# First attention layer of an eight-layer hybrid network: two-part normalization, loads in another order and in slices, and TensorE's transposes and products in groups of one or two steps

## The chip, the cores and the metric

The kernel runs on one core of one Trainium2 chip. The metric is the device time of one execution in microseconds (us): the median of several runs. A separate execution is recorded by the hardware profiler, and every duration below comes from that one execution unless it is called a median. A core has five engines that run side by side, each taking its own queue of instructions in order: TensorE (PE, matrix products and transposes, with PEld for its weight loads), VectorE (DVE), ScalarE (ACT), GpSimd (POOL) and SyncE (SP, which only issues transfers here). Transfers (DMA) run on 16 DMA engines, which all issuing queues share. TensorE writes only to PSUM; VectorE and ScalarE copy its results out to SBUF.

## The reference, cut to what matters

The network is eight layers with residuals on an input x of 4 sequences x 1024 positions x 128 features, all in float32. The change concerns the first layer, a causal attention with 16 heads of 64 features:

```python
x = x + _L0_attn_a_ref(_layernorm(x, axis=-1), Wq, Wk, Wv, Wo, bo)
...
def _L0_attn_a_ref(x, Wq, Wk, Wv, Wo, bo):
    q = split_heads(x @ Wq)
    k = split_heads(x @ Wk)
    v = split_heads(x @ Wv)
    scores = jnp.einsum('bhid,bhjd->bhij', q * beta, k)
    ...
    scores = jnp.where(causal, mask_value, scores)
    attn = jax.nn.softmax(scores, axis=-1)
    out = jnp.einsum('bhij,bhjd->bhid', attn, v)
    out = out.transpose(0, 2, 1, 3).reshape(b, n, INNER)
    return out @ Wo + bo
```

After it come a mixture of experts, a gated attention, the mixture again, a state-space layer, a gated feed-forward layer, a second attention and the feed-forward layer again. Their arithmetic does not change.

## The kernel before, in words

**The constructors load the weights.** `LOADS` (L1706) lists the layers in the order in which their constructors run. Nearly all loads go to SP's queue. `GatedAttention.relative_bias` (L802) builds a table through a round trip to DRAM: POOL fills `rel_row`, SP writes it out (L823) and reads it back shifted (L825). `GatedFFN.scaled` loads three integer weights, each into a short-lived buffer, and POOL converts them (L1286). The short-lived buffers reuse each other's memory, and the attention's working tiles come to lie on it too. `load_late` (L91) puts the mixture's two large weights W1 and W2 (2 MB each) in a list `k.late`, after one exponential of the state-space layer; the attention issues the whole list on ACT's queue (L371 to L375) when it has reached query group 2 of the first pair of heads.

**Units.** The attention works on 32 pairs of heads: 4 sequences x 8 pairs. The 1024 queries of a pair are cut into four groups `gq` = 0 to 3 of two blocks of 128 (`Q` = 2, `NQ` = 4). Being causal, group `gq` needs the first 2(gq+1) key blocks, so its second stage has gq+1 *steps* of two key blocks. That makes 10 steps a pair, and 36 pairs of (key block, query block) on or under the diagonal, of which a step holds 4, or 3 on the diagonal.

**First stage**, `probabilities` (L336), a generator: for each query block, matrix products give the scores `s` of both heads (L352, each head on its 64 rows of the array); DVE adds the mask, writes `p` and finds the maximum (L358, and L365 if there were two tiles); ACT takes the exponential and its sum (L367). After the second block of a unit DVE takes the reciprocal `r` of the sums (L380). The factors are then needed along another axis: SP writes `r` to DRAM (L383) and reads it back, broadcast, with two transfers (L386) into `share`.

**Second stage**, `outputs` (L414): in each step, TensorE transposes the two key blocks of `p` (L426, into tiles `t`), DVE and ACT copy one each to `pt` (L433, L431), and `product` (L447) multiplies by the values (L451, each head into its 64 columns of the array) and sums in `o`; after the last step DVE multiplies `o` by `share` (L458). The products of a step are kept in `waiting` and issued one step later.

**Small work**, `pieces`: projections of a later pair (`projected`, L265: two features each of q and k, evacuated by ACT at L282 and by DVE at L284, and four pieces of values for every second pair, L291, evacuated by L107 and L109 in turn), the output projection of the pair before (`joined`, L306), and the turning of the normalized input (L260). All of them use one PSUM tile, `m` of pool `ps_m`. `outputs` issues one piece in each step. `ahead` (L402) then runs the first stage until it is `LEAD` = 20 blocks ahead.

So TensorE's order, which is written out by hand (`pe` pins it), is in each step: transposes, one piece, scores, products of the step before. `ve` pins the order of DVE's score reductions; other instructions are placed in their engine's queue by a scheduler, which can deviate from the order of the source. [...]in tiles of 128 x 512 float32, `ps_s` has 2 x 2, `ps_t` 2 x 1, `ps_o` and `ps_m` one each, eight in all.

**Between sequences**, `normalized(b)` (L248) is called two pairs before the next sequence begins: `normalize` (L111) does the statistics (L117, L119) on DVE, a square root on ACT (L121), then reciprocal and scaling on DVE (L122, L124), and appends the two pieces that turn the result.

Of the kernel before, what the change touches and what calls it, by code (L numbers as in the profile page):

```python
# [11 lines left out]
F32 = mybir.dt.float32  # L12
# [8 lines left out]
P = 128  # L21
B = 4
# [39 lines left out]
class Kernel:  # L62


    def __init__(self, ctx: ExitStack, tc: tile.TileContext, ins: dict, out):
# [5 lines left out]
        self.got = ctx.enter_context(tc.tile_pool(name="got", bufs=GOT))  # L71
# [19 lines left out]
    def load_late(self, pool, name, shape, src):  # L91

        t = pool.tile(shape, F32, name="w_" + name)
        self.late.append(lambda: self.nc.scalar.dma_start(t, src))
        return t
# [15 lines left out]
    def normalize(self, out, in_, n=NC, pin=lambda ins: ins):  # L111
# [9 lines left out]
        nc.scalar.activation(rstd, mv[:, :, 1], AF.Sqrt, bias=self.eps)  # L121
        pin(nc.vector.reciprocal(rstd, rstd))  # L122
# [72 lines left out]
class AttentionA:  # L195
# [10 lines left out]

    Q = 2
    NQ = NC // 2
    LEAD = 20
# [11 lines left out]
    def __call__(self, start=None):  # L221
# [4 lines left out]
        with self.stack as ctx:  # L226
# [4 lines left out]
            ps_s = ctx.enter_context(tc.tile_pool(name="a_ps", bufs=2, space=PSUM))  # L231
            ps_t = ctx.enter_context(tc.tile_pool(name="a_pt", bufs=2, space=PSUM))
# [12 lines left out]
            xts, pairs, units = {}, {}, {}  # L245
            pieces = []

            def normalized(b):  # L248
                xl = one.tile([P, NC, C], F32, tag="xl", name="xl")
                k.normalize(xl, k.xb(b), pin=ve)  # L250
                nc.gpsimd.tensor_tensor(
                    k.xb(b), k.xb(b), bo.unsqueeze(1).to_broadcast([P, NC, C]), ALU.add
                )

# [81 lines left out]
            def probabilities(n, gq):  # L336
# [7 lines left out]
                for i in range(Q):  # L344
# [67 lines left out]
            waiting = []  # L412

            def outputs(n, gq):  # L414


                p, share = units.pop((n, gq))
                last = (gq + 1) * Q - 1
                for step in range(gq + 1):
                    products = []  # L420
                    for jb in (2 * step, 2 * step + 1):
                        lo = max(0, jb * P - gq * Q * P)
                        t = ps_t.tile([P, 2, Q * P], F32, tag="t", name="t")
                        for h in range(2):
                            for i in range(lo // P, Q):
                                pe(nc.tensor.transpose(  # L426
                                    t[:, h, i * P : (i + 1) * P], p[:, h, i, jb * P : (jb + 1) * P], k.ident
                                ))
                        pt = sb.tile([P, 2, Q * P], F32, tag=f"pt{jb % 2}", name="pt")
                        if jb % 2:  # L430
                            nc.scalar.copy(pt[:, :, lo:], t[:, :, lo:])  # L431
                        else:
                            nc.vector.tensor_copy(pt[:, :, lo:], t[:, :, lo:])  # L433
                        products.append((jb, lo, pt))
                    done[1] += 4 if step < gq else 3
                    if pieces:
                        pieces.pop(0)[1]()
                    ahead()
                    while waiting:
                        waiting.pop(0)()  # L440
                    if step == 0:
                        o = ps_o.tile([P, Q * P], F32, tag="o", name="o")
                    waiting.append(
                        lambda products=products, step=step: product(n, gq, o, share, products, last, step == gq)
                    )

            def product(n, gq, o, share, products, last, at_end):  # L447
                for jb, lo, pt in products:
                    for h in range(2):
                        feats = slice(h * DH_A, (h + 1) * DH_A)  # L450
                        pe(nc.tensor.matmul(  # L451
                            o[feats, lo:], pairs[n]["v"][:, jb, feats], pt[:, h, lo:],
                            start=jb == 0, stop=jb == last,
                        ))
                if at_end:
                    if gq == 0:
                        pairs[n]["o"] = sb.tile([P, T], F32, tag="ot", name="ot")
                    nc.vector.tensor_tensor(  # L458
                        pairs[n]["o"][:, gq * Q * P : (gq + 1) * Q * P], o, share, ALU.mult
                    )  # L460

            normalized(0)
# [12 lines left out]
            while waiting:  # L475
                waiting.pop(0)()
# [8 lines left out]
class Mixture:  # L485
# [7 lines left out]
    def __init__(self, k: Kernel):  # L493
# [15 lines left out]
        self.place = w.tile([P, CAP], F32, name="place")  # L509
        nc.gpsimd.iota(  # L510
            self.place, [[1, CAP]], base=0, channel_multiplier=0, allow_small_or_imprecise_dtypes=True
        )
# [10 lines left out]
    def __call__(self, start=None):  # L523
# [1310 lines left out]
```

## Time and profile before

| | us |
|---|---|
| median of 3 runs (3391.43 to 3402.13) | 3398.55 |
| the profiled execution, total | 3378.53 |
| its span, from the first to the last instruction | 3376.7 |
| last product of the first attention (L451) starts | 1214.03 |

The profiled execution is 20.0 us, or 0.6%, quicker than the median of the runs.

| stretch of the span | length | PE busy | DVE busy | ACT busy | granted TensorE clock |
|---|---|---|---|---|---|
| 0 to 30 us | 30 | 15.77 | 11.03 | 9.17 | 1.00 |
| 100 to 200 us | 100 | 100.00 | 68.47 | 53.73 | 1.00 |
| 500 to 600 us | 100 | 96.21 | 69.23 | 53.51 | 0.97 |
| 800 to 900 us | 100 | 95.03 | 70.86 | 54.40 | 0.98 |

The busy times are sums over the instructions of an engine in the stretch. TensorE's ends are modelled, so that instructions of a run overlap in the record and "100.00" says that there is always some instruction, not that the array computes all the time; the distance from one start to the next is what is measured. The clock is the mean share of full speed that the throttle granted. A line of an engine's timeline gives start, length, engine, line, operation, output<-input, count, and in brackets the idle time before it with what ended it.

### The profile page before, as it was taken

To read this page: it belongs to the slowest core of one execution; us is meant where nothing else is said; L and a number is where in the kernel's file an instruction comes from. 1 tells how busy PE (TensorE), PEld (TensorE's weight loads), DVE (VectorE), ACT (ScalarE), POOL (GpSimd) and SP (SyncE) were. 2 spreads that over 40 slices of the span, in tenths; PEclk is the share of its full clock that TensorE was granted. 3 is DMA by queue.
4 is the path that set the end of the run, shared out by engine and by line. 5 is a ranking of instruction groups with operands and counts; after the bars stand their busy time and mean duration, and the time that the engine had idled before them with its cause. 6 is when DMAs were issued, how large, how long until landed. Compare 5 with 4: busy or idle time off the path is not lost.

```text
span 3376.7 us, 45533 instructions
## 1 busy us (share of the span) xinstructions
PE 3015.2 (89%) x16624; PEld 1655.0 (49%) x16624; DVE 2306.0 (68%) x5281; ACT 1812.9 (54%) x3819; POOL 273.0 (8%) x269
## 2 busy tenths in 40 slices
PE   5999999999999979869988597978778799999988
PEld 2555555555455547635566344444445344444435
DVE  3666666666776656666566589897977677677634
ACT  2555555555555523445423597979654265556662
POOL 1000000000000002530013200000001101010000
PEclk8999999999999989989999798989999699899999
DMA  5110111111110101100001111111111112121100
GB/s 156 16 16 14 15 18 16 14 17 17 14 17 15 15 8 32 53 10 1 0 16 40 53 64 50 57 57 51 63 38 42 34 44 53 31 51 31 30 2 25
DMA packets 149537, 109.35 MB, mean 32 GB/s; under 512 B 91760, under 2 KB 130432, under 8 KB 146880
## 3 DMA queue, kind: packets, MB, share of 16 engines
q1 hardware_dynamic: 128352, 72.84, 9.4%
q0 software_dynamic: 17408, 27.32, 3.3%
q10 hardware_dynamic: 3552, 6.29, 0.6%
q8 instruction: 130, 2.13, 0.4%
q14 instruction: 95, 0.78, 0.1%
HBM read 90.76 MB, written 15.60 MB: 31 GB/s over the span
## 4 chain that ended last, share of the span: by engine, by line
PE 68%; DVE 11%; ACT 8%; DMA 6%; issue 6%; POOL 1%; SPq 0%; DVEq 0%; ACTq 0%; POOLq 0%
PE s L352 8%; PE t L426 8%; PE o L451 8%; PE acc L649 4%; PE o L1613 4%; PE acc L1227 4%; PE x L1579 3%; PE ps L280 3%; PE acc L948 3%; PE s L1515 3%; ACT p L1585 3%; DMA shares<-r 2%; ACT hc L1226 2%; DVE st L1214 2%; DVE tops L1524 2%
## 5 line engine op out<-in xcount | busy, mean ns | idle before, releaser
L358 DVE CUSTOM_DVE_ANT_0 p<-s,mask 128x512 f32<-128x512 f32 (+3 forms) x768 | 394.6, 553 | 170.5 <-PE s L352 168.3
L367 ACT ACTIVATE p<-p,tops 128x640 f32<-128x640 f32 (+7 forms) x512 | 391.7, 767 | 146.1 <-DVE tops L365 85.4
L1585 ACT ACTIVATE p<-x 128x512 f32<-128x512 f32 (+3 forms) x768 | 337.6, 490 | 246.4 <-PE x L1584 176.6
L1524 DVE TENSOR_REDUCE tops<-s 128x2 f32<-128x1024 f32 (+3 forms) x384 | 361.3, 956 | 133.8 <-PE s L1520 94.2
L431 ACT COPY pt<-t 128x512 f32<-128x512 f32 (+1 forms) x320 | 157.7, 493 | 380.0 <-PE t L426 379.5
L1227 PE MATMUL acc<-hc,ident 128*128 128x512 f32 x512 | 270.1, 652 | 93.2 <-ACT hc L1226 92.3
L352 PE MATMUL s<-kt,qt 64*128 64x512 f32 (+3 forms) x1536 | 339.4, 533 | 2.7 <-DVE tops L358 2.6
L451 PE MATMUL o<-pt,vv 128*64 128x256 f32 (+1 forms) x2560 | 323.3, 374 | 14.7 <-ACT pt L431 9.4
L426 PE MATMUL t<-ident,p 128*128 128x128 f32 x2304 | 326.2, 282 | 3.7 <-DVE pt L433 3.0
L426 PEld LDWEIGHTS t<-ident,p 128*128 128x128 f32 x2304 | 248.1, 142 | 103.3 <-issue 70.0
L1214 DVE TENSOR_TENSOR_SCAN st<-decay,st 128x1024 f32<-128x1024 f32 x128 | 288.8, 2279 | 10.9 <-ACT decay L1211 10.4
L451 PEld LDWEIGHTS o<-pt,vv 128*64 128x64 f32 x2560 | 156.6, 137 | 263.9 <-issue 157.3
L433 DVE COPY pt<-t 128x512 f32<-128x512 f32 x320 | 220.0, 687 | 66.0 <-PE t L426 66.0
L1579 PE MATMUL x<-q,k 75*128 75x512 bf16 (+3 forms) x768 | 223.1, 338 | 27.7 <-ACT p L1585 15.0
L1515 PE MATMUL s<-k,q 72*128 72x512 bf16 (+3 forms) x768 | 216.3, 348 | 31.9 <-DVE tops L1524 17.6
L1226 ACT ACTIVATE hc<-ps,by_time 128x256 f32<-128x256 f32 x512 | 200.7, 478 | 50.6 <-PE ps L1220 50.5
L352 PEld LDWEIGHTS s<-kt,qt 64*128 64x128 f32 x1536 | 112.5, 188 | 180.7 <-issue 139.7
L1227 PEld LDWEIGHTS acc<-hc,ident 128*128 128x128 f32 x512 | 91.7, 198 | 209.6 <-ACT hc L1226 191.0
L738 POOL DMA_INDIRECT got<-y_rows,rows x128 | 136.7, 1068 | 645.1 <-DMA y_rows<-y 543.5
L1213 DVE TENSOR_TENSOR st<-du,bs 128x1024 f32<-128x1024 f32 x128 | 151.8, 1217 | 49.4 <-PE ps L1220 49.2
L649 PE MATMUL acc<-d,xl 128*128 128x480 f32 (+1 forms) x384 | 152.8, 559 | 26.2 <-DVE d L644 26.2
L1220 PEld LDWEIGHTS ps<-ident,st 128*128 128x128 f32 x1024 | 126.0, 146 | 96.5 <-issue 60.7
(272 smaller groups left out, 4740.7 us busy)
## 6 DMA issues: line engine op xcount, KB each, us to landing
bs<-b_rows SPq DMA_DIRECT2D x64, 512.0 KB
share<-shares SPq DMA_DIRECT2D x256, 64.0 KB
k<-b_parts POOLq DMA_DIRECT2D x16, 576.0 KB, 13.2
q<-b_parts POOLq DMA_DIRECT2D x48, 192.0 KB, 12.1
b_parts<-part SPq DMA_DIRECT2D x24, 256.0 KB
y_rows<-y SPq DMA_DIRECT2D x16, 192.0 KB
x<-in_x_dram SPq DMA_DIRECT2D x4, 512.0 KB
w_W<-in_W_dram ACTq DMA_DIRECT2D x1, 2048.0 KB
```

The lines of the kernel that those rows point to most:

```text
L352: pe(nc.tensor.matmul(s[:, h, : hi - lo], q[feats, ib * P : (ib + 1) * P], kk[feats, lo:hi], start=True, stop=True,))
L358: ve(nc.vector.tensor_tensor_reduce(p[:, h, i, lo:hi], s[:, h, : hi - lo], m, -1.0, 3.4e38, ALU.add, ALU.min, tops[:, h, i, at : at + 1],))
L367: exp = nc.scalar.activation(p[:, h, i, :width], p[:, h, i, :width], AF.Exp, bias=tops[:, h, i, 0:1], scale=-1.0, accum_out=sums[:, h, i : ...
L426: pe(nc.tensor.transpose(t[:, h, i * P : (i + 1) * P], p[:, h, i, jb * P : (jb + 1) * P], k.ident))
L451: pe(nc.tensor.matmul(o[feats, lo:], pairs[n]["v"][:, jb, feats], pt[:, h, lo:], start=jb == 0, stop=jb == last,))
L649: pe(nc.tensor.matmul(acc[n][:, :m, :].rearrange("p e s -> p (e s)"), xl[:, c, :], d[:, e : e + m, :].rearrange("p e s -> p (e s)"), start ...
L1214: nc.vector.tensor_tensor_scan(st, decay, st, 0.0, ALU.mult, ALU.add)
L1227: nc.tensor.matmul(acc[:, c : c + 2, :].rearrange("p c d -> p (c d)"), k.ident, hc.rearrange("p c d -> p (c d)"), start=n == 0, stop=n == ...
L1515: start.pin(nc.tensor.matmul(s[:, a, : hi - lo], qq[:ROWS, two + a, ib * P : (ib + 1) * P], kk[:ROWS, two + a, lo:hi], start=True, stop=ha ...
L1524: nc.vector.tensor_reduce(tops[:, half, two : two + 2, n], s[:, :, : hi - lo], AX.X, ALU.max)
L1579: start.pin(nc.tensor.matmul(x[:, lo:], kk[:FULL, a, jb * P : (jb + 1) * P], qq[:FULL, a, hq * 512 + lo : (hq + 1) * 512], start=True, sto ...
L1585: nc.scalar.activation(p[:, a, lo:], x[:, lo:], AF.Exp)
```

## The change

The diff has these parts. `normalize` becomes a generator `normal` with a break after the square root; in the attention, statistics and root run three pairs ahead at `gq` 1, the scaling at `gq` 2, and the two turning pieces (`across`) are appended where the whole was before. `GatedFFN` moves ahead of `GatedAttention` in `LOADS`. `load_late` makes one transfer for each of the 8 experts instead of one for all, and one entry of the list is issued at the end of each unit from unit 2 on. In the second stage, transposes and products come in groups, `GROUPS`: six a pair instead of ten steps. A group issues a piece, all its transposes, another piece, the products of the group before, and then calls `ahead`. The transposed tiles, now of two key blocks, share a ring of three buffers with the scores (`ps_s` with 3 x 2 tiles, `ps_t` gone), and the copies `pt` have 4 buffers for each of their two tags instead of 2. The mixture's gather buffers and its table `place` move from the constant pool into the mixture's own pools.

```diff
@@ Kernel
-        self.got = ctx.enter_context(tc.tile_pool(name="got", bufs=GOT))
...
-        self.late.append(lambda: self.nc.scalar.dma_start(t, src))
+        self.late.extend(
+            lambda at=at: self.nc.scalar.dma_start(t[:, at], src[:, at]) for at in range(shape[1])
+        )
...
-    def normalize(self, out, in_, n=NC, pin=lambda ins: ins):
+    def normalize(self, out, in_, n=NC):
+        for _ in self.normal(out, in_, lambda ins: ins, n):
+            pass
+    def normal(self, out, in_, pin, n=NC):
...
         nc.scalar.activation(rstd, mv[:, :, 1], AF.Sqrt, bias=self.eps)
+        yield
         pin(nc.vector.reciprocal(rstd, rstd))
@@ AttentionA
+    GROUPS = [[(0,)], [(0, 1)], [(0,), (1, 2)], [(0, 1), (2, 3)]]
...
-            ps_s = ctx.enter_context(tc.tile_pool(name="a_ps", bufs=2, space=PSUM))
-            ps_t = ctx.enter_context(tc.tile_pool(name="a_pt", bufs=2, space=PSUM))
+            ps_s = ctx.enter_context(tc.tile_pool(name="a_ps", bufs=3, space=PSUM))
...
-                k.normalize(xl, k.xb(b), pin=ve)
+                parts = k.normal(xl, k.xb(b), ve)
+                next(parts)
+                yield
+                for _ in parts:
+                    pass
...
-                    if k.late and gq == 2:
+                    if k.late and i == Q - 1 and n * NQ + gq > 1:
                         pin = k.order()
                         pin(exp)
-                        while k.late:
-                            pin(k.late.pop(0)())
+                        pin(k.late.pop(0)())
...
             def outputs(n, gq):
                 p, share = units.pop((n, gq))
+                for steps in self.GROUPS[gq]:
+                    piece()
+                    blocks = [block for step in steps for block in turned(p, gq, step)]
+                    piece()
+                    while behind:
+                        behind.pop(0)()
+                    if steps[0] == 0:
+                        o = ps_o.tile([P, Q * P], F32, tag="o", name="o")
                     ahead()
+                    behind.append(lambda blocks=blocks: products(n, gq, o, share, blocks))
...
+            def turned(p, gq, step):
+                t = ps_s.tile([P, 2, 2, Q * P], F32, tag="s", name="t")
...
+                    blocks.append((jb, lo, sb.tile([P, 2, Q * P], F32, tag=f"pt{m}", name="pt", bufs=4)))
+                for m, (jb, lo, pt) in enumerate(blocks):
+                    if m:
+                        nc.scalar.copy(pt[:, :, lo:], t[:, m, :, lo:])
+                    else:
+                        nc.vector.tensor_copy(pt[:, :, lo:], t[:, m, :, lo:])
+                done[1] += 4 if step < gq else 3
...
                 for gq in range(NQ):
+                    if gq == 1 and n + 3 < B * NP and (n + 3) % NP == 0:
+                        normal = normalized((n + 3) // NP)
+                    if 0 < gq < 3:
+                        next(normal, None)
                     if gq == 0 and n + 2 < B * NP and (n + 2) % NP == 0:
-                        normalized((n + 2) // NP)
+                        across((n + 2) // NP)
@@ Mixture
-        self.place = w.tile([P, CAP], F32, name="place")
...
+            many = ctx.enter_context(tc.tile_pool(name="m_got", bufs=GOT))
...
+            place = one.tile([P, CAP], F32, name="place")
...
-LOADS = [AttentionA, GatedAttention, GatedFFN, StateSpace, AttentionB, Mixture]
+LOADS = [AttentionA, GatedFFN, GatedAttention, StateSpace, AttentionB, Mixture]
```

More of the change, by code (lines that the diff above doesn't have):

```diff
@@ L244, in __call__ @@
             )
-            xts, pairs, units = {}, {}, {}
+            xls, xts, pairs, units = [], {}, {}, {}
             pieces = []
@@ L253, in normalized, with across @@
                 )
+                xls.append(xl)
+            def across(b):
+                xl = xls.pop()
                 def turned(h):
@@ L410, in ahead, with piece @@
                         break
-            waiting = []
+            def piece():
+                if pieces:
+                    pieces.pop(0)[1]()
+            behind = []
             def outputs(n, gq):
                 p, share = units.pop((n, gq))
[L418 to L437, printed above, removed]
-                    ahead()
[L439 to L445, printed above, removed]
@@ L447, in product @@
-            def product(n, gq, o, share, products, last, at_end):
-                for jb, lo, pt in products:
-                    for h in range(2):
[L450 to L460, printed above, removed]
@@ L462, in __call__ @@
-            normalized(0)
+                for steps in self.GROUPS[gq]:
[6 more added lines that the diff above has]
+                        o = ps_o.tile([P, Q * P], F32, tag="o", name="o")
+                    ahead()
+                    behind.append(lambda blocks=blocks: products(n, gq, o, share, blocks))
@@ new lines, in products @@
+            def products(n, gq, o, share, blocks):
+                for block in blocks:
+                    product(n, gq, o, *block)
+                if blocks[-1][0] < (gq + 1) * Q - 1:
+                    return
+                if gq == 0:
+                    pairs[n]["o"] = sb.tile([P, T], F32, tag="ot", name="ot")
+                nc.vector.tensor_tensor(
+                    pairs[n]["o"][:, gq * Q * P : (gq + 1) * Q * P], o, share, ALU.mult
+                )
+            def turned(p, gq, step):
+                t = ps_s.tile([P, 2, 2, Q * P], F32, tag="s", name="t")
+                blocks = []
+                for m in range(2):
+                    jb = 2 * step + m
+                    lo = max(0, jb * P - gq * Q * P)
+                    for h in range(2):
+                        for i in range(lo // P, Q):
+                            pe(nc.tensor.transpose(
+                                t[:, m, h, i * P : (i + 1) * P], p[:, h, i, jb * P : (jb + 1) * P], k.ident
+                            ))
+                    blocks.append((jb, lo, sb.tile([P, 2, Q * P], F32, tag=f"pt{m}", name="pt", bufs=4)))
[5 more added lines that the diff above has]
+                done[1] += 4 if step < gq else 3
+                return blocks
@@ L463, in __call__, with product @@
+            def product(n, gq, o, jb, lo, pt):
+                for h in range(2):
+                    feats = slice(h * DH_A, (h + 1) * DH_A)
+                    pe(nc.tensor.matmul(
+                        o[feats, lo:], pairs[n]["v"][:, jb, feats], pt[:, h, lo:],
+                        start=jb == 0, stop=jb == (gq + 1) * Q - 1,
+                    ))
+            normal = normalized(0)
+            for _ in normal:
+                pass
+            across(0)
             projected(0)
@@ L474, in __call__ @@
                     outputs(n, gq)
-            while waiting:
-                waiting.pop(0)()
+            behind.pop(0)()
             joined(B * NP - 1)
@@ L508, in __init__ @@
         )
-        self.place = w.tile([P, CAP], F32, name="place")
-        nc.gpsimd.iota(
-            self.place, [[1, CAP]], base=0, channel_multiplier=0, allow_small_or_imprecise_dtypes=True
-        )
         self.before = w.tile([P, P], F32, name="before")
@@ L539, in __call__ @@
             xls, spots = {}, {}
+            place = one.tile([P, CAP], F32, name="place")
+            nc.gpsimd.iota(
+                place, [[1, CAP]], base=0, channel_multiplier=0, allow_small_or_imprecise_dtypes=True
+            )
             def normalized(b):
@@ L644, in dispatch @@
                     ve(nc.vector.tensor_tensor(
-                        d, ex.place.unsqueeze(1).to_broadcast(shape),
+                        d, place.unsqueeze(1).to_broadcast(shape),
                         spot[:, c, :].unsqueeze(2).to_broadcast(shape), ALU.is_equal,
@@ L736, in fetch @@
                     c, n = pairs[i]
-                    got[i] = k.got.tile([P, C], F32, tag="got", name="got")
+                    got[i] = many.tile([P, C], F32, tag="got", name="got")
                     nc.gpsimd.indirect_dma_start(
```

## The prediction

> **What bounds the kernel now.** I read the granted clock and busy times by stretch first, then the chain of waits in one pair of heads, then single places in the timeline. By stretch (length; PE, PEld, DVE, ACT, POOL busy with counts; clock; DMA share; GB/s):
>
> ```profile
> 30.00:60.00 30.00, 14.28 (x60) 8.11 (x60) 7.72 (x31) 7.51 (x20) 2.35 (x2) 0.77 0.56 153
> 60.00:100.00 40.00, 34.52 (x160) 16.80 (x160) 19.00 (x56) 15.22 (x36) 0.00 (x0) 0.79 0.13 27
> 200.00:300.00 100.00, 96.21 (x588) 50.63 (x587) 69.77 (x224) 50.54 (x114) 2.35 (x1) 0.98 0.10 17
> 400.00:500.00 100.00, 100.00 (x622) 53.32 (x618) 68.77 (x212) 53.84 (x129) 0.00 (x0) 1.00 0.16 17
> ```
>
> TensorE is the bound from about 85 to 1215 us; the start is something else; and each 100 us in which a sequence begins (200, 500, 800) runs 583 to 592 matmuls where others run about 622. The chain inside a pair (start, length) is TensorE alone:
>
> ```profile
> 418.07 0.80 PE o L451 x8
> 418.87 1.03 PE t L426 x8
> 419.90 0.86 PE ps L280 x2
> 420.76 1.06 PE s L352 x4
> 421.82 1.01 PE o L451 x8
> ```
>
> Each run has a part that grows with its work and a part that doesn't. Eight transposes take 1.02, six 0.80 to 0.81: 0.107 each, 0.17 left over. A full step's products take 1.01, a diagonal one's (a quarter less work) 0.80: 0.85 is work, 0.16 left over; at the stage's end two steps in one run take 1.66 instead of 1.01 + 0.80, so the second entry of 0.15 vanishes. Scores 512, 384 and 256 wide take 1.06, 0.85, 0.63: 0.21 left over. A piece, 0.86, shows none. So a step holds 0.53 us in which the array changes over, 5.3 in the ten steps of a pair. Check: 72 x 0.107 + 36 x 0.213 (products) + 36 x 0.213 (scores) + 8 pieces x 0.86 = 29.9, plus 5.3 = 35.2; measured 35.4 (below).
>
> SP's queue in the same pair:
>
> ```profile
> 412.06 2.12 SPq L383 DMA_DIRECT2D shares<-r  x2
> 420.94 2.37 SPq L386 DMA_DIRECT2D share<-shares  x4
> 423.41 0.53 SPq L383 DMA_DIRECT2D shares<-r  x1
> 433.15 1.08 SPq L386 DMA_DIRECT2D share<-shares  x2
> 434.29 0.58 SPq L383 DMA_DIRECT2D shares<-r  x1
> 444.69 1.08 SPq L386 DMA_DIRECT2D share<-shares  x2
> 447.47 2.01 SPq L383 DMA_DIRECT2D shares<-r  x2
> ```
>
> The doubled write recurs after 35.41 us, the period of a pair. SP waits out each write before the read; it is full except for some 4 us a pair: a second limit close behind TensorE.
>
> **The start.** Timeline rows of two engines:
>
> ```profile
> 50.28 0.02 ACT L94 MOVE_SHAPE w_W<-in_W_dram  x1 [17.23 <-DMA w_b<-in_b_dram]
> ...
> 60.91 0.42 DVE L458 TENSOR_TENSOR ot<-o,share 128x256 f32<-128x256 f32 x1 [7.49 <-DMA share<-shares]
> ```
>
> ACT stands 17.23 us while W1 and W2 are issued, and the copies behind it hold TensorE 9.42 us. The first `r` is ready at 27.96, but SP issues it at 36.09, behind all loads; with W1 in the DMA queues it takes 14.4 us, and `o` is free at 60.91. *After*: the three conversions run first (issue 11.6; landing and conversion 5.0 + 1.2, 2.35 + 1.2, 2.5 + 1.2: about 25), then POOL's rows (2.4) and the round trip of the table (4.2): 32; read-back and the other loads, two more: SP gets to the first write at about 34. A write takes 9.0 in the steady part (97 of them), the reads 3 to land: 46 to 47 instead of 60.91, **14 us**. Next, the before issues pair 1's four features in a row (69.6 to 80.6 for 4 x 0.86 of work, each waiting for the evacuation of the one tile `m`); the change pops them in the four slots of group 2, **7 us**. About 3 us of half-clock runs go too (products x8 at 1.97 instead of 1.08). Sum 24. Lower end 10 (SP reaches the write no earlier than before). Upper end 35: by 100 us 260 matmuls are done, 42 us at the later rate, so 58 are lost, and some 22 of these (load, normalize, first scores) stay.
>
> **W1, W2 in 16 slices** on ACT, one a unit: ACT's issues took 0.38 and 0.88; 17 x 0.88 = 15 us of queue over 17 units, beside ACT's 46% idle time; without that cover, 15. Taken as 1. Behind each wait exponentials and copies needed a group later.
>
> **Normalization.** TensorE waits for the scaled rows at each new sequence:
>
> ```profile
> 285.07 1.24 PE L260 MATMUL ps<-ident,xl 128*128 128x128 f32 x4 [3.79 <-DVE xl L124]
> ```
>
> From the transposes before to this piece it is 4.67, otherwise 0.71: 3.96 lost, and the next scores (2.08 for 1.13) and turning (1.24 for 0.60) run at half clock, about 1.6 in all: 5.6 x 3 = 17. (35, 31 and 40 missing matmuls at 6.2 per us say the same: 17.) After, this is done 20 us early. What stays: DVE's bursts of 1.6 + 0.6 and 0.2 + 2.1 us, and ACT's root with two table loads of 1.28. They stand before score reductions, which have a slack of about 2 us in the ring; I take 0.5 us each, 6 x 0.5 = 3 (ends 0 and 9). POOL's add (2.35) finds POOL idle. Net **-14**.
>
> **Groups.** Six a pair instead of ten. A group has the same three changes of the array (scores to whole array, whole array to column halves, to row halves), 0.53, and two new seams, piece to transposes and back. Here a rule helps: "Mode switching requires drain: Changing tiling mode (not just tile) drains the TensorE" (the Trainium skill, TensorEngine Tiling (Array Packing), Key Properties). By it a seam within the whole array is free: 6 x 0.53 = 3.2, 2.1 saved a pair, 66 us in the 31 pairs after the first. By the row a run of transposes followed by a piece starts it 0.93 after, not 0.85: 0.07 a seam, 6 x 0.67 = 4.0, 1.3 saved, 40 us. The seams lie in between, as some have no piece: 0.60, 3.6, 1.7 saved: **-53**.
>
> Against it stand new waits. (a) The ring. In group (1,2) of `gq` 2, scores two and three need the buffers of the two transposed tiles, and ACT's copy of the second stands behind two exponentials of 1024 (1.14 each). With T' the end of the 512 scores before: reductions and minimum to T'+1.6, exponentials to T'+4.0, copy (0.35) to T'+4.4; the third scores could start at T'+3.55. 0.95 us. (b) The tile `m`. Two pieces of a group are separated only by its transposes, 0.64 to 1.7, where a whole step lay before. The evacuation of the first waits behind the last reductions or exponentials: in (0,1) of `gq` 3, 0.3; in `gq` 0, for pairs with values, 0.85 (reductions of 512 and 256 first), so 0.4 on average; in (0,) of `gq` 2, 0.35, so 0.2. Together 1.85. Lower end 0: queues do not keep the source's order (at 401.25 a copy stands ahead of ready exponentials), DVE idles 31%. I take 1.3, two thirds: 31 x 1.3 = **+40**. Net -13; with the ends, -66 to +17.
>
> **Rest.** The tail: the last scores lie later in the order, and the last share needs 14 us from `r` as before: +2. `place` is made on an idle POOL, 20 us before use. The gather buffers now lie where the next layer's tiles come, but those are written only after the last gather (1457.8): at 1461 at the earliest; 0 to +3, taken as 0.
>
> **Sum.** -24 + 1 - 14 - 13 + 2 = -48: 3378.5 becomes 3330 as profiled. The median lies 20 us above that execution, so I take the difference off the median: 3398.55 - 48 = 3350.
>
> **Rivals.**
>
> *Waits eat the groups* (twice what I take in one place, none elsewhere, or all of 1.85): groups +5, sum -30: 3368. For it: one `m`, one ring. Against: the idle shares.
>
> *Groups in full, no waits*: -53 or more and -24 - 14 + 3: 3310, to 3295 at the upper ends. For it: before, TensorE waited almost nowhere. Against: two pieces a group.
>
> *SP becomes the bound: slower.* A trip costs 9.1 + 1.24 + 0.1; the doubled one 8.7 + 3.4 + 0.1: 33.1 a pair, under my 35.0. The doubling exists because the `r` of `gq` 3 and of the next `gq` 0 come 1.75 us apart (411.85, 413.60). After, the exponentials again follow each other on ACT, by my order 1.9 us apart, 2.5 with a copy between. If the doubling breaks, four trips take 41.8 us, above TensorE's period, and `o` waits for `share`: (41.8 - 35.4) x 31 = +198, less the start's and normalization's 38: 3555. It decides from the point where SP's trips add up to more than a pair's period. A rule would dismiss it: about 2.0 us fixed per DMA (the Trainium skill, DMA: Bandwidth & Descriptors, Anatomy of one DMA, measured on another issuing path): 4 x (2.0 + 1.8) = 15 us a pair, never a bound. The row says 9.0 for these writes of single 4-byte elements, so it stays alive.
>
> *Waits above 3 us a pair*, the same mechanism as (a) and (b) at several places: 3405 and up.
>
> **How the numbers follow.** Forecast 0.46; waits eat it 0.22; groups in full 0.17; SP bound 0.10; larger waits 0.05. The range takes in the first three: 3298 from the full groups with a better start, 3395 from eaten groups with the start at its lower end. A measurement tells about 0.3%, 10 us, from no change. Faster: nearly all of the first three, 0.82; same 0.04; slower 0.14.
>
> **What would show it.** Right: no L94 wait on ACT near 50 us, the first `ot` at 47, no 3.8 us before L260, six runs of transposes a pair, a period of 34.5 to 35.2 us. The waits: transposes or scores on TensorE ended by L431 or L433, pieces by L282, L284 or L107. SP: `x1` writes only, and `ot` ended by share. Wrong: a period above 35.4, or new waits in later layers by their tiles on the gather buffers.

## The result: slower by 2.4%, and where the time went

The changed kernel takes 3479.84 us (median of 4 runs, 3477.48 to 3480.73) against 3399.33 for the kernel before: a ratio of 1.0243, 95% interval 1.0224 to 1.0262. The forecast was 3350, range 3298 to 3395; it lies on the wrong side. The two profiled executions differ by more than the medians, 3478.7 against 3376.7 us of span, because the one of before was 20 us under its own median.

The same stretches as before, in the changed kernel (columns as above: length; PE, PEld, DVE, ACT, POOL busy with counts; clock; DMA share; GB/s):

```profile
30.00:60.00 30.00, 19.97 (x96) 11.20 (x94) 13.70 (x47) 11.42 (x28) 2.27 (x4) 0.89 0.64 89
60.00:100.00 40.00, 37.56 (x232) 21.93 (x230) 25.96 (x77) 20.10 (x47) 0.00 (x0) 1.00 0.20 35
200.00:300.00 100.00, 88.99 (x564) 51.58 (x564) 65.12 (x214) 48.55 (x114) 2.36 (x1) 1.00 0.13 19
400.00:500.00 100.00, 94.93 (x608) 56.36 (x608) 67.10 (x212) 51.31 (x125) 0.00 (x0) 1.00 0.11 16
```

The start is better: 328 matmuls between 30 and 100 us instead of 220. After that TensorE no longer runs through: 608 matmuls where before had 622, and 564 instead of 588 in the stretch from 200 us.

The last multiply of each pair of heads gives the pair's period. Before, the quiet pairs alternate between 34.37 and 36.35 us, mean 35.36. After, they alternate between 36.35 and 36.05, mean 36.20. Besides, pairs 2 to 5 take 47.8, 40.8, 41.6 and 40.0, pairs 13 and 25 take 40.0 and 39.1, and pairs 21, 22, 24 and 28 between 41.5 and 44.8.

TensorE in one quiet pair of the changed kernel (timeline rows; in brackets the idle time before the row and what ended it):

```profile
416.06 1.13 PE L335 MATMUL ps<-ot,w_Wo 128*128 128x512 f32 x2 [0.38 <-DVE sum_t L337]
...
423.64 0.92 PE L369 MATMUL s<-kt,qt 64*128 64x384 f32 x4 [0.18 <-DVE tops L375]
424.49 1.12 PE L297 MATMUL ps<-xt,w_Wq 128*128 128x512 f32 x2
425.45 1.91 PE L470 MATMUL t<-ident,p 128*128 128x128 f32 x16
428.57 1.12 PE L297 MATMUL ps<-xt,w_Wk 128*128 128x512 f32 x2 [1.21 <-ACT qt L299]
```

At 427.36 the second piece of the group (L297) cannot start: the one tile `m` still holds the first until ScalarE has copied it out (its evacuation). ScalarE's rows say why that is late:

```profile
424.97 0.40 ACT L384 ACTIVATE p<-p,tops 128x128 f32<-128x128 f32 x1
...
427.33 0.61 ACT L384 ACTIVATE p<-p,tops 128x384 f32<-128x384 f32 x1
427.93 0.58 ACT L299 ACTIVATE qt<-ps 128x512 f32<-128x512 f32 x1
```

Six exponentials, from 424.97 on, stand ahead of it. SyncE's queue shows what happens in pairs 2 and 3:

```profile
130.69 1.32 SPq L402 DMA_DIRECT2D share<-shares  x2
132.07 0.58 SPq L399 DMA_DIRECT2D shares<-r  x1
141.16 1.09 SPq L402 DMA_DIRECT2D share<-shares  x2
142.30 0.59 SPq L399 DMA_DIRECT2D shares<-r  x1
151.41 2.40 SPq L402 DMA_DIRECT2D share<-shares  x2
153.86 0.59 SPq L399 DMA_DIRECT2D shares<-r  x1
163.35 1.08 SPq L402 DMA_DIRECT2D share<-shares  x2
```

Only single writes: four round trips of about 10.7 us a pair, back to back. A doubled write, two writes in a row and then their four reads, would save one trip. 25 of the 31 places where one pair ends and the next begins have one (place 3 lies between pairs 2 and 3; before has 30, all but the first); places 1 to 4, 22 and 25 have none. At place 3 both `r` were there before SyncE issued the first of their writes at 153.86 (VectorE):

```profile
149.62 0.18 DVE L396 RECIPROCAL r<-sums 128x4 f32<-128x4 f32 x1 [0.25 <-ACT p L384]
151.77 0.17 DVE L396 RECIPROCAL r<-sums 128x4 f32<-128x4 f32 x1
```

Still the second write came at 164.48, behind the read of the first. So SyncE takes its queue in the order that it was given, and that order lacks the doubling here.

Later, the state space layer begins with a stop of 26.86 us where before had 5.44 (ScalarE, before and after, then TensorE after):

```profile
1881.68 1.28 ACT L1156 ACT_TABLE_LOAD   x1 [5.44 <-PE ps L1150]
```

```profile
1976.81 1.28 ACT L1191 ACT_TABLE_LOAD   x1 [26.86 <-DVE x L784]
```

```profile
1978.84 2.07 PE L1185 MATMUL ps<-xt,w_taps 128*128 128x512 f32 x2 [19.94 <-ACT u L1191]
```

L784 is the mixture's addition of the gathered rows. My reading is that the tile `u` lies on the moved gather buffers and waits until they have been read; two runs below test it.

### The profile page after: what moved, and what is told of

Read it like the earlier page. It is cut to its first block, busy times and chain, and to the rows that moved or that the text cites. A ratio compares the mean times of both kernels' runs of the same rounds, so it can differ in the third digit from the quotient of the medians.

```text
span 3478.7 us, 45483 instructions
## 1 busy us (share of the span) xinstructions
PE 3011.2 (87%) x16624; PEld 1713.3 (49%) x16624; DVE 2302.4 (66%) x5281; ACT 1808.5 (52%) x3822; POOL 272.0 (8%) x270
## 4 chain that ended last, share of the span: by engine, by line
PE 33%; DVE 9%; ACT 7%; issue 5%; DMA 2%; POOL 1%; another core or an unknown queue 0%; DVEq 0%; ACTq 0%; POOLq 0%; SPq 0%
PE acc L1262 4%; PE o L1648 4%; PE x L1614 3%; PE s L1550 3%; PE acc L983 3%; ACT p L1620 3%; ACT hc L1261 2%; PE acc L684 2%; DVE st L1249 2%; DMA b_parts<-part 2%; DVE tops L1559 2%; PE ps L1255 1%; PE ps L998 1%; PE ps L1356 1%; PE py L717 1%
## 5 line engine op out<-in xcount | busy, mean ns | idle before, releaser
L369 PE MATMUL s<-kt,qt 64*128 64x512 f32 (+3 forms) x1536 | 314.6, 522 | 9.2 <-DVE tops L375 5.7
L485 PE MATMUL o<-pt,vv 128*64 128x256 f32 (+1 forms) x2560 | 298.6, 372 | 21.2 <-DVE ot L457 21.2
L470 PEld LDWEIGHTS t<-ident,p 128*128 128x128 f32 x2304 | 259.1, 141 | 100.1 <-issue 70.1
L470 PE MATMUL t<-ident,p 128*128 128x128 f32 x2304 | 288.4, 275 | 6.7 <-DVE tops L375 3.9
L485 PEld LDWEIGHTS o<-pt,vv 128*64 128x64 f32 x2560 | 169.6, 139 | 182.5 <-issue 71.4
L478 DVE COPY pt<-t 128x512 f32<-128x512 f32 x320 | 211.5, 683 | 7.1 <-PE t L470 6.6
L369 PEld LDWEIGHTS s<-kt,qt 64*128 64x128 f32 x1536 | 123.5, 191 | 112.2 <-issue 66.9
L1648 PE MATMUL o<-p,vx 128*32 128x512 f32 (+3 forms) x1536 | 172.8, 522 | 0.0
```

The costliest lines, as they stand in the source:

```text
L369: pe(nc.tensor.matmul(s[:, h, : hi - lo], q[feats, ib * P : (ib + 1) * P], kk[feats, lo:hi], start=True, stop=True,))
L470: pe(nc.tensor.transpose(t[:, m, h, i * P : (i + 1) * P], p[:, h, i, jb * P : (jb + 1) * P], k.ident))
L485: pe(nc.tensor.matmul(o[feats, lo:], pairs[n]["v"][:, jb, feats], pt[:, h, lo:], start=jb == 0, stop=jb == (gq + 1) * Q - 1,))
L1648: start.pin(nc.tensor.matmul(o[a * VW : (a + 1) * VW, lo:], vx[b % 2][:, jb, first : first + VW], p[:, a, lo:], start=jb == 0, stop=jb == ...
```

## The experiments

The runs were made on several chips, on which the kernel before itself took 3376 to 3471 us (medians). So each result is a ratio to runs of before on the same chip:

| kernel | ratio | 95% interval |
|---|---|---|
| the change | 1.0243 | 1.0224 to 1.0262 |
| b_pools | 1.0075 | 1.0052 to 1.0099 |
| b_start | 1.0044 | 1.0032 to 1.0057 |
| a_sharepool | 1.0197 | 1.0165 to 1.0230 |
| a_single | 1.0679 | 1.0642 to 1.0715 |
| a_trips | 1.0142 | 1.0107 to 1.0177 |
| b_trips | 0.9969 | 0.9953 to 0.9985 |
| a_trips_single | 1.0406 | 1.0366 to 1.0446 |
| a_trips_piece | 1.0103 | 1.0061 to 1.0145 |
| a_rbufs | 1.0044 | 1.0026 to 1.0063 |
| a_fix | 0.9996 | 0.9975 to 1.0017 |
| b_rbufs | 0.9921 | 0.9891 to 0.9951 |
| a_wact | 1.0298 | 1.0276 to 1.0320 |
| a_notrip | 1.0070 | 1.0046 to 1.0093 |
| b_notrip | 0.9968 | 0.9954 to 0.9982 |
| a_notrip_piece | 0.9896 | 0.9873 to 0.9918 |
| b_rbufs_again | 0.9934 | 0.9912 to 0.9956 |
| a_short | 1.1409 | 1.1370 to 1.1448 |
| b_short | 1.0827 | 1.0792 to 1.0862 |

Names with a_ start from the changed kernel, those with b_ from the kernel before.

### The mixture's buffers

**b_pools** is the kernel before with this part of the change alone:

```diff
-        self.got = ctx.enter_context(tc.tile_pool(name="got", bufs=GOT))
...
+            many = ctx.enter_context(tc.tile_pool(name="m_got", bufs=GOT))
```

> The kernel before with only the mixture's gather buffers and its row of places moved into the mixture's own pool; nothing in the first attention changes. Theory: the tile of the state space layer that now lies on the gather buffers waits for the last gather, and the mixtures lose as well: 25 to 40 us slower, 3425 to 3440, with a stall of some 27 us on ScalarE ahead of the first table load of the state space layer. Rival: the 36 us that the later layers lost are a difference between two executions (the profiled run of before was 20 us under its own median): within 5 us of 3399, and no such stall.

Measured +0.75%, 26 us by the ratio and 21 between the medians, and the same stop as after the whole change, in a kernel whose attention is untouched:

```profile
1923.49 1.28 ACT L1156 ACT_TABLE_LOAD   x1 [26.83 <-DVE x L749]
```

**a_fix** changes nothing but the order of the mixture's pools, on top of a_rbufs (below):

```diff
+            many = ctx.enter_context(tc.tile_pool(name="m_got", bufs=GOT))
             one = ctx.enter_context(tc.tile_pool(name="m_one", bufs=1))
             sb = ctx.enter_context(tc.tile_pool(name="m_sb", bufs=2))
-            many = ctx.enter_context(tc.tile_pool(name="m_got", bufs=GOT))
```

> a_rbufs with the mixture's gather buffers allocated ahead of its other tiles instead of behind them, so that another tile of the layer after lies on them. Theory, the place of the buffers: the state space layer no longer starts with a wait of some 20 to 27 us for the last gather, 18 to 25 us under a_rbufs. Rival, another tile that is needed as early comes to lie there: within 5 us of a_rbufs.

From 1.0044 to 0.9996: 13.4 us between the medians, less than expected; the stop is 5.58 us, where a_rbufs had 26.90. So the place of the buffers causes this stop, and another place removes it: from its first to its last instruction on TensorE, the state space layer takes 704.6 us in a_rbufs and 683.8 in a_fix; b_rbufs (below), with the buffers unmoved and on the same chip, takes 683.9.

Part of the cost stays, and the place cures only this stop. On the same chip and by the same measure, the gated attention between the two mixtures takes 278.0 us in b_pools, 280.7 in a_rbufs and 281.4 in a_fix, against 274.1 in b_start and 272.6 in b_rbufs, where the buffers are unmoved. Here ScalarE waits 21.1 us for the same addition in the changed kernel (23.5 in a_fix) and holds TensorE 21.9 us. Before has a stop of 24.7 in this layer too, behind another tile, so only 4 to 9 us are lost. That the buffers' place causes this as well was not tested.

### The round trips of the shares

**b_start** is the kernel before with the new order of loads and the slices of W1 and W2.

> The kernel before with only the reordered loads and W1 and W2 loaded in 16 slices. Theory: the gain at the start is its own and stays: the first multiply of a share at about 47 instead of 61 us, the last products of the attention 12 to 20 us earlier, 3380 to 3387 in all. Rival: SyncE's round trips are a second limit so near that the gain of the start is taken back while W1 and W2's slices hold up the writes of the shares: pairs of the first 250 us longer than 36.4 us, total 3395 to 3405.

The gain at the start is there, but the rival held, and more: 0.44% slower. Pair 0 ends at 98.6 instead of 106.0 us, but pairs 2 to 4 take 44.4, 39.2 and 39.5 us instead of 34.4, 36.4 and 34.4. SyncE's rows, of before and then of this kernel:

```profile
120.76 2.12 SPq L383 DMA_DIRECT2D shares<-r  x2
```

```profile
122.75 0.59 SPq L384 DMA_DIRECT2D shares<-r  x1
134.81 1.08 SPq L387 DMA_DIRECT2D share<-shares  x2
136.32 0.36 SPq L384 DMA_DIRECT2D shares<-r  x1
145.11 1.08 SPq L387 DMA_DIRECT2D share<-shares  x2
```

Before doubles the write at place 2; here the second write, at 122.75, stands behind a read, and places 1, 2 and 4 have no doubling. As at place 3 of the changed kernel, the order was in the queue from when the kernel was built: the second `r` of place 2 was ready at 115.38. This kernel has the new loads and the slices of W1 and W2 together, so which of the two moves the order stays open. Places 1 to 4 do lie in the stretch in which ScalarE issues the slices (62.8 to 192.4 us here, 63.1 to 195.9 in the changed kernel); places 22 and 25 of the changed kernel do not.

**a_sharepool**: the changed kernel with the two reads on GpSimd's queue.

```diff
-                            nc.sync.dma_start(
+                            nc.gpsimd.dma_start(
                                 share[h * DH_A : (h + 1) * DH_A],
```

> The changed kernel with only the two reads of each share issued from GpSimd's queue, so that SyncE's queue no longer waits out each write before the next one. Theory: the pairs of 39 to 48 us are SyncE's chain of four single round trips of some 10.5 us; with it broken they fall to about 36.5, some 40 us in all: 3435 to 3445. Rival: these pairs have another cause (the order on ScalarE and VectorE): 3475 to 3485, pairs of 40 us and more remain.

In between (1.0197). Pairs 2 and 3 fall from 47.8 and 40.8 to 38.0 and 36.1, but others grow (9 and 16 to over 41), and it is not a clean test: reads can land late from there. Four issued from 426.12 us on moved most of their data from 436 to 438, and the multiply ran at 438.38:

```profile
438.38 0.42 DVE L457 TENSOR_TENSOR ot<-o,share 128x256 f32<-128x256 f32 x1 [5.52 <-DMA share<-shares]
```

**a_trips** leaves the queues as they are and fixes only the order on SyncE's:

```diff
-                        nc.sync.dma_start(there.rearrange("h i p -> p h i"), r)
+                        sp(nc.sync.dma_start(there.rearrange("h i p -> p h i"), r))
...
-                        for h in range(2):
+                        held.append((share, there))
+                        if gq < NQ - 1 or n == B * NP - 1:
```

> The changed kernel with one thing held in order on SyncE's queue: the reads of the share of gq 3 come after the write of the next pair's gq 0, so that the queue has three round trips a pair everywhere (in the changed kernel some pairs have three, those of the first 250 us and a few later ones four). Theory, SyncE's order: the pairs of 40 to 48 us fall to 36.2 (those of a new sequence to 38 or 39), the attention ends 40 to 50 us earlier, 3430 to 3440 in all. Rival, the orders on ScalarE and VectorE make these pairs long: 3465 to 3480.

1.0142: 1.0% less than the change, about 34 us. In the profile the attention ends 26 us earlier, not 40 to 50: the theory holds for a part of the long pairs. Pairs 3, 4 and 22 fall from 40.8, 41.6 and 44.8 to 36.0, 37.9 and 37.5, and the attention's last multiply from 1266.4 to 1240.3 us. Pairs 5, 13 and 21 (new sequences) and 2, 24 and 28 stay at 40 to 43.

**b_trips** puts the same order, the loads and the two-part normalization into the kernel before.

> The kernel before with the reordered loads and slices, the two-part normalization and the three round trips held in order, but with its own second stage, its own buffers and the mixture's pool unmoved. Theory: the gain at the start (7 to 19 us) and at three new sequences (5 to 14) stay once no pair has four trips: 3370 to 3390. Rival: the normalization's gain is hidden or the gain at the start is lost in another place: 3395 to 3415.

0.9969, 10 us faster than before. Whether that is the start's gain is not shown: pair 0 ends at 98.8 instead of 106.0 us, but pairs 1 to 4 take 152.3, where before takes 141.4. The pairs around a new sequence (5 and 6, 13 and 14, 21 and 22 together) take 76.1, 71.6 and 75.3 instead of 78.4, 78.5 and 79.1. VectorE's waits show the next limit: `r` has two buffers and waits for the write of the one two units back (total, times, longest; before had 36.8 in 20):

```profile
DVE r L397 <- DMA shares<-r: 67.6, 27, 5.4
```

**a_rbufs**, **b_rbufs**: `r` in four buffers, on top of a_trips_piece (below) and of b_trips.

```diff
-                        r = sb.tile([P, 2, Q], F32, tag="r", name="r")
+                        r = sb.tile([P, 2, Q], F32, tag="r", name="r", bufs=4)
```

> a_trips_piece with one more thing: the tile r (16 bytes a partition) in four buffers instead of two, so that VectorE's reciprocal doesn't wait for the write of the r two units before. Theory, r's buffers: the pairs of 38 to 41 us with stops of TensorE of 3 to 8 us come from VectorE standing in the reciprocal (57.8 us in 25 waits between 45 and 1210 us); they fall below 37, 25 to 40 us under a_trips_piece. Rival, the round trip itself is too long: the waits move to the multiply by the share, within 10 us of a_trips_piece.

> b_trips (the kernel before with the reordered loads, the two-part normalization and three round trips a pair) with the tile r in four buffers. Theory, r's buffers: its waits of 67.6 us in 27 go and with them the pairs of 37 to 40 us without a new sequence, 12 to 25 us under b_trips, a ratio to before of 0.990 to 0.993. Rival: the waits move to the multiply by the share, within 6 us of b_trips.

In both, the waits for `r` are gone. The multiply's waits for its share grew from 62.9 (17 times) to 161.2 us (43) in the first and from 21.1 (6) to 83.1 (23) in the second: theory and rival are each half right. These two ran on another chip than the kernels that they build on, and a write took longer there: 10.29 us in a_rbufs, 9.63 in a_trips_piece (medians of the 66 single writes, from issue to the read behind it). The ratios still fall, by 0.6 and 0.5%. b_rbufs was then run once more:

> b_rbufs once more. Theory, the length of a write decides how much the trips cost: where the writes take the 9.0 us of the first profile instead of 10.1, the pairs of 39 to 46 us without a new sequence shrink, and the ratio to before is 0.990 or lower. Rival: the ratio stays at 0.992 whatever the writes take.

There a write took 8.72 (9.93 in the run before), the pairs of over 37.5 us (pair 21 left out) went from nine to one, but the ratio stayed, 0.9934. That before suffers from long writes as much would fit, as its own median fell from 3470.7 to 3375.8 us; no profile of before on these chips shows it. b_rbufs is the best whole kernel of this study, 22 to 27 us faster than before.

**a_wact**: a_fix with the writes on ScalarE's queue and no order held by hand.

> a_fix with the writes of the shares on ScalarE's queue and the reads alone on SyncE's, without an order held by hand, so that no trip queues behind another. Theory, the trips are still too near each other: up to 15 us under a_fix. Rival, ScalarE pays for 128 more issues (0.4 to 0.9 us each in its queue) and for waiting on r: 10 to 40 us above a_fix.

Much worse than theory and rival, 1.0298: every pair but the last takes 38 to 46 us. The write doesn't get shorter (issued at 648.75, read issued at 658.27), and the multiply waits for its share for 195.5 us in all. Why the whole pair slows was not settled.

### Groups, single steps and the tile for pieces

**a_single** and **a_trips_single** give each step its own group, without and with the held order:

```diff
-    GROUPS = [[(0,)], [(0, 1)], [(0,), (1, 2)], [(0, 1), (2, 3)]]
+    GROUPS = [[(0,)], [(0,), (1,)], [(0,), (1,), (2,)], [(0,), (1,), (2,), (3,)]]
```

> The changed kernel with the ten steps of a pair each in a group of its own (still products a group behind, still up to two pieces a group). Theory: grouping saves its 1.7 us of changes of the array, and its waits on the ring of three and on the one tile for pieces cost some 2.5: the undisturbed pairs go from 36.2 to 35.4 or less, and 3450 to 3465 in all. Rival: the waits come from the two pieces around each turning and the shared ring, not from groups of two: undisturbed pairs of 37 to 38 us, 3500 or more.

> The changed kernel with three round trips a pair as in a_trips, and each of the ten steps of a pair in a group of its own. Theory, SyncE's order: the 3629 us of the single steps were pairs with four trips (its queue had only five doubled writes); now the pairs take some 37.3 and the whole 1.2 us a pair more than a_trips, 3465 to 3485. Rival, single steps with two pieces each are slow by themselves: above 3540.

In a_single (1.0679) only 4 of the 31 places have a doubled write, and most pairs take 41 to 50 us. The held order returns 2.7%, not the 4 to 5% expected, and ends at the edge of the rival: the odd pairs then take 37.3 to 37.8, the even ones 41.2 to 46.1 (pairs 5, 13, 21 and the last two left out); in pair 8, 3.6 us are stops for the tile `m`. So single steps in this order are slow with the trips held too, and groups of two make that better, not worse: a_trips has 36.04 and 36.35.

**a_trips_piece** moves the second piece:

```diff
                     blocks = [block for step in steps for block in turned(p, gq, step)]
-                    piece()
                     while behind:
                         behind.pop(0)()
+                    piece()
```

> a_trips with the second piece of a group moved from before to behind the products of the group before. Theory, the one tile for pieces: the stops of TensorE for its evacuation (1.77 and 1.95 us in two pairs looked at) fall below 0.5 us a pair, against up to 0.9 us for one more change of the array in each group: 15 to 40 us under a_trips. Rival, the changes of the array cost as much as the stops: within 10 us of a_trips.

1.0103 against 1.0142, 14 us between the medians, just under the low end and within overlapping intervals, so this run alone decides nothing. The odd quiet pairs do fall to 35.77 and one even one, 20, to 33.74; others wait for shares.

**a_notrip**, **b_notrip** and **a_notrip_piece** leave out the writes (every `share` is read from a table of ones), to see the second stage alone:

```diff
-                        there = dram.tile([2, Q, P], F32, tag="shares", name="shares")
-                        nc.sync.dma_start(there.rearrange("h i p -> p h i"), r)
```

> The changed kernel with the shares taken from a table of ones that is written once at the start: the 128 writes of r are left out, so the output isn't the reference's, and no pair can wait for a round trip. Theory: what stays of the loss is the second stage itself (36.2 us a pair where before had 35.4) and the mixture's buffers: every pair without a new sequence is within 1 us of 36.2, a ratio to before of 1.003 to 1.010. Rival: pairs of 40 us and more remain without any trip, ratio 1.014 or more.

> The kernel before with the same table of ones in place of the 128 writes (its output isn't the reference's). Theory: before is bound by TensorE and loses little to the trips, at the start and in two or three pairs: 10 to 25 us faster, ratio 0.9925 to 0.997; the changed kernel without trips is then 25 to 50 us slower than this one, which is what groups, normalization and buffers cost together. Rival, the groups are a gain that only the trips hide: the changed kernel without trips is as fast as this one or faster.

> a_notrip (no writes of r, output not the reference's) with the second piece of a group behind the products. Theory, the one tile for pieces: the stops for its evacuation go, the pairs alternate between some 33.8 and 35.8 us, mean 34.8, 30 to 45 us under a_notrip. Rival: the order brings other stops (scores behind the reductions): less than 15 us under it.

These are the clearest runs. In a_notrip the long pairs 2 to 4, 22 and 28 are gone: 36.35, 36.05, 36.35, 36.23, 36.35. What stays above is 38.3 in pairs 8 and 16, 39.9 in 24 and 40.0 to 44.2 at new sequences. b_notrip has before's 34.37 and 36.35. The changed kernel is slower without trips too, by 1.0%. Then one moved piece returns 1.7%, 58 us between the medians, more than expected: pairs of 33.65 and 35.77, mean 34.71, and 640 matmuls where the change had 608:

```profile
400.00:500.00 100.00, 99.46 (x640) 57.57 (x636) 69.34 (x217) 53.51 (x130) 0.00 (x0) 1.00 0.05 17
```

The waits of TensorE for `m` between 45 and 1210 us (total, times, longest), in a_notrip:

```profile
PE ps L301 <- ACT qt L303: 45.7, 30, 8.9
...
PE ps L339 <- DVE sum_t L343: 5.2, 11, 1.2
```

and in a_notrip_piece:

```profile
PE ps L339 <- DVE sum_t L343: 0.8, 1, 0.8
PE ps L301 <- ACT qt L303: 0.7, 1, 0.7
```

The 8.9 us lie at the start (54.9 us). With the trips, the same move returned only 14 us: a_trips_piece lies 2.1% above a_notrip_piece, so at pairs as short as 34.7 us even three trips cost time.

### A short write

**a_short** and **b_short** let TensorE turn `r` first, so that the write is of 4 rows instead of 512 single elements:

```diff
-                        nc.sync.dma_start(there.rearrange("h i p -> p h i"), r)
+                            pe(nc.tensor.transpose(ps[: 2 * Q, :P], r.rearrange("p h i -> p (h i)"), k.ident))
+                            nc.vector.tensor_copy(share[: 2 * Q, :P], ps[: 2 * Q, :P])
+                            nc.sync.dma_start(there, share[: 2 * Q, :P])
```

> The changed kernel with the second piece behind the products, the gather buffers first and r in four buffers, and in place of the write of 512 single elements one turn of r by TensorE (four rows of 128) as one more piece a unit, so that the write is of 4 rows. Theory, the 9 to 10 us are the single elements: the write falls to 2 to 5 us, no pair waits for its share, and the four turns cost 0.3 us each: pairs of some 35 to 36 us, a ratio to before of 0.985 to 0.995. Rival, the write's time is fixed and not by its elements: it stays near 9 us, the trips are four a pair again, and the ratio is 1.00 or more.

> The kernel before with the reordered loads, the two-part normalization, r in four buffers and the same turn of r by TensorE ahead of a write of 4 rows. Theory: no pair waits for its share, but four more turns a pair stand in the way of TensorE, which had no stops: pairs of 36 to 37 us, a ratio to before of 0.99 to 1.00, behind a_short. Rival: the write stays near 9 us, ratio 1.00 or more.

The first half of the theory holds: the read, which waits for the write to land, follows 1.17 us after the write's issue, not 9.

```profile
409.62 0.25 SPq L405 DMA_DIRECT2D shares<-share  x1
410.79 1.08 SPq L407 DMA_DIRECT2D share<-shares  x2
```

The second half falls: the turn stands in TensorE's queue before its `r` is ready, and everything behind it waits.

```profile
409.01 0.27 PE L403 MATMUL ps<-ident,r 128*4 128x128 f32 x1 [4.06 <-DVE r L396]
```

That is 252.6 us in 88 waits in a_short, where nearly all pairs take 51 to 54 us, and 150.5 in 98 in b_short. The turn would have to be put later; that was not tried, so whether the 0.9896 can be had with trips stays open.

## Why the prediction was wrong

The runs without trips divide the loss:

| part | us | from |
|---|---|---|
| round trips of the shares | +48 | 0.0243 less (1.0070 - 0.9968), of 3399 |
| place of the gather buffers | +26 | b_pools, 0.0075 of 3399 |
| pairs 1 to 29 without trips | +24 | 1072.7 in a_notrip, 1049.0 in b_notrip |
| start without trips | -15 | pair 0 ends at 87.7, not 103.0 |
| sum | +83 | measured: +80 |

The first line is a difference of three ratios, good to some 10 us; the second to 8. As the first is what the other lines must leave over, the sum tests only these: 26 + 24 - 15 = 35, and the ratios of the two kernels without writes differ by 1.0%, 35 us. Of the 48, a_trips returned 34 by holding the order; 14 stay, as the trips cost 24 us even in the held order (1.0142 less 1.0070) and 11 before (1 less 0.9968).

**The step that failed first is the rival "SP becomes the bound", put at 0.10.** Its mechanism, price and point of decision were right: four single trips, 41.8 us a pair forecast, 40.0 to 47.8 measured. I argued it away by the order and spacing of two `r` on ScalarE, 1.9 to 2.5 us by my own reckoning, as if SyncE paired them when they came. That spacing is 2.0 us at the 25 doubled places, as forecast, and 2.1 to 3.1 at the six others; but the doubling is missing there although both `r` were ready in time (place 3), because the queue's order is fixed beforehand. It was therefore no case of all or nothing: it costs where the order lacks a doubling, and in pairs nearby. The case for all pairs was priced at 198 us (its total adds up to 3559, not 3555); what came is 48.

**"The gather buffers now lie where the next layer's tiles come ... taken as 0"**: 26. I looked only at the handover to the gated attention. The one to the state space layer, after the second mixture, has the stop of 26.86 us; and the gated attention loses 4 to 9 us as well (b_pools, a_rbufs and a_fix), where I had allowed 0 to 3. The stated sign, "new waits in later layers by their tiles on the gather buffers", is what the profile shows.

**Groups, -53.** TensorE without its stops takes 34.28 and 34.41 us in pairs 9 and 10, where before took 36.3 and 34.4 without any: 1.0 saved, not 1.7, so -31. **New waits, +40.** The stops are 1.77 and 1.95 us in these two pairs, so +58. Of the two kinds, (a) was put too high (0.18 for 0.95) and (b) too low: in the group (0,1) of `gq` 3 the wait is 1.21, not 0.3. I had let the evacuation wait behind the last exponentials, not behind six. The net is +27 instead of -13. The waits add up to those of the rival "waits eat the groups" (all of 1.85), though they are others than it named; its groups came to +5 because it kept the full saving, and it had nothing for trips and buffers. That the stops and not the groups' work make the net is what a_notrip_piece shows: without them the changed kernel's pairs are 0.65 us shorter than before's, 34.71 against 35.36.

**Start, -24.** -18.6 in the changed kernel (pair 0 ends at 87.4 instead of 106.0), within its ends. SyncE's first write at 34.27 and read at 44.63 came as forecast; the first multiply came at 53.2, not 47, as its read took 8.6 us to reach the multiply, not 3. In the DMA queues at that time is the read-back of the gated attention's table (960 KB, issued at 36.58, moving until 49.4); the first slice of W1 comes at 63.08. That this read-back is what held the share up was not tested. But b_start shows that this gain alone is lost again within four pairs.

**Normalization, -14.** No stop of 3.8 us before the turns (L277 after). Counted over the three pairs around a new sequence, against three quiet ones: 6.5 us lost in b_notrip each time; 3.8, 3.8 and 8.0 in a_notrip. So -4. What stays is in good part stops for `m` again (4.2 us in pair 5 of a_notrip, 1.6 in the quiet pair 9); in a_notrip_piece the losses are 2.4, 2.4 and 3.0.

The sums of the views before were not at fault; TensorE was the bound, with SyncE 2 us of slack behind it. What was missing is that both slacks, SyncE's and that of the one tile, were used up by orders that I took from the source.

## What to carry to other kernels

A queue that waits out each write runs in the order that the kernel was built with, whatever is ready first: count its round trips in the new order before trusting that they fit, and hold the order by hand if they only just do. A saving on the engine that is the bound is worth what its single-buffered tile lets through: put the two uses of such a tile as far apart as the order allows. When a buffer moves to another pool, follow every layer whose tiles can come to lie on it, not only the next.

## What the runs showed of the hardware

A write of 512 single elements of 4 bytes took 9.09 us from issue to the read behind it (before, median of the 66 single writes, 7.35 to 13.12), one of 4 rows of 512 bytes 1.16 (a_short, median of 128). The same kernel's writes took 9.93 us on one chip and 8.72 on another (b_rbufs twice), and the kernel before took 3470.7 and 3375.8 us in these two comparisons. Four reads of shares issued from GpSimd's queue moved most of their data about 10 us after the issue (a_sharepool, from 426.12).
